# Moving two reloads, one normalization and the opening of an attention stage inside a hand-ordered four-layer graph kernel

## The chip, the cores and the metric

The kernel runs on one core of a Trainium2 chip, as one launch, in float32 throughout. The metric is the device time of one execution in microseconds (us). A core has a matrix engine (PE, with its weight loads shown apart as PEld), a vector engine (DVE), a scalar engine (ACT), a general engine (POOL) and a queue that mainly issues DMA transfers (SP). Each takes its instructions in the order in which the program lists them, and they wait for one another through semaphores.

## The reference, cut to what matters

The input x has 128 batches of 64 tokens with 256 features. Four layers follow one another. Each begins with a layer norm and a relu and adds its result to x:

```python
# layer 0: aggregation with a normalized adjacency, then two dense layers with batch norms
x = x + gnn0(relu(layernorm(x)), adj, W1, ..., W2, ...)
# layer 1: two graph convolutions, then LSTMs over windows of 1, 2, 3, 4 tokens
h = relu(einsum('ts,bsh->bth', adj, relu(layernorm(x)) @ Wg0 + bg0))
h = relu(einsum('ts,bsh->bth', adj, h @ Wg1 + bg1))
for p in range(1, 5):
    last = lstm_last(Wih[p-1], Whh[p-1], ..., windows of p tokens of h)
    h = h.at[:, every p-th token, :].set(last)
x = x + h
# layer 2: causal attention with one head; layer 3: attention with four heads, masked by adj
x = x + attention2(relu(layernorm(x)), Wqkv, Wo)
x = x + attention3(relu(layernorm(x)), W, adj)
```

The four LSTMs run one after the other: that of length 2 reads what that of length 1 wrote. Layer 0's batch norms need sums over the whole batch, so layer 0 ends everywhere before layer 1 begins anywhere.

## The kernel before, in words

The 8192 tokens are cut into 16 chunks of 512 (`NCH`), and two chunks make a superchunk (`SUP`), of which there are 8, numbered 0 to 7. Most large products are done with seven block products in place of eight, with sums and differences of blocks on DVE and POOL; that is where names such as `xd` (differences of an operand) and `hd` come from.

Three stretches follow one another. The first is layer 0. The second, from about 240 us to about 1525 us of the profile, is layer 1: one superchunk at a time goes through the LSTMs of length 1, 2, 3 and 4 (`single`, line 1346, and `lstm`, line 1072). The third is the two attentions.

**The places of a superchunk.** `single` and `lstm` are generators. They list the LSTM's instructions and stop (`yield`) at places where other work may be listed. The loop at lines 1597 to 1632 counts the places of a superchunk from 0 to 21, with half places in between: 0 to 3 are in the LSTM of length 1, 4 to 7 in that of length 2, 8 to 13 in that of length 3 and 14 to 21 in that of length 4. At each place it advances the generators that are due there. Since the engines take instructions in listed order, a place fixes what is ahead of what on every engine.

**What is placed.** `convolutions` (line 1001) prepares a chunk for its LSTMs in 17 steps. In the order of the steps it: scales the stored result of layer 0 (line 918, DVE); transposes it and writes it to memory in HBM (`put`, line 261, into `far_y`); reads it back in another layout (`get`, line 268, four transfers of 128 KB into a `cv` tile) and loads the chunk of x (line 1017, 512 KB into `xs`); adds the two (`add_squares`, line 298, two DVE instructions); takes the layer norm's sums in two halves (`norm_halves`, lines 195 to 203, with the factors on POOL at the end); applies the norm in two halves on ACT (line 210); and goes on with the convolutions' products. The `put` writes out the tile that `xs` then takes over.

`BEGUN` gives the places of the first steps for the two chunks of the superchunk after the next: eight steps for its first chunk, four for its second. `CONV` gives the places of the other steps, one superchunk later; `FIRST` (the tuple at line 1561) does so for superchunk 0, where nothing was begun ahead. The steps of BEGUN run in superchunks 0 to 5, so twelve chunks are begun in this way.

**The queue that they share.** All these transfers, and the LSTMs' weights, are issued by SP in listed order. `load_sets(2)` (line 905) issues two weight sets `wset` of 896 KB each; it stands twice in the last time step of every LSTM of length 2 to 4: between places 11.5 and 12 and again between 12 and 13 for length 3, and between 19.5 and 20 and again between 20 and 21 for length 4. There are six buffers for such sets. `residual` (line 1304) adds the LSTMs' result to x and `ahead` (line 1495) prepares attention; both put and get through SP as well.

**The opening of attention.** After layer 1 the order is written as lists of steps. The string `FIRST` (line 2054) opens it: its entries name a step and a chunk, as `score2+2` is the masked score of layer 2 for chunk 2, `divide2`, `turn2` and `out2` are the softmax's division, its transposes and the product with v, `norm3`, `apply3` and `chan3` are layer 3's norm sums, its application (with one DVE instruction, line 185, and four on ACT, line 187) and the transposes to channels, `q30`, `k30`, `q31`, `k31` are layer 3's projections (line 1529), and `res1` and `pair1` are the last steps of layer 1's residual for chunks 14 and 15. `THIRD` follows, with the first round of the steady order.

Of the kernel before, what the change touches and what calls it, by code (L numbers as in the profile page):

```python
# [19 lines left out]
def kernel(  # L20
# [1443 lines left out]
    def new_hT(sc):  # L1464

        hTs[sc] = l1r.tile([P, KD, SUP * CH], F32, tag="hT", name=f"hT_{sc}")
# [89 lines left out]
    EARLY = 0, 3, 5, 7, 9, 9, 13, 15  # L1556
    RESIDUAL = (0, 6, 9), (5.5, 7, 9.5)
    CONV = (3, 4, 5, 5.5, 7, 8, 9, 10, 10), (5, 5, 6, 9.5, 11, 11.5, 13, 14, 15, 15.5, 17, 18, 20)
    BEGUN = (11, 11.5, 13, 14.5, 17, 17, 20, 21), (17.5, 19, 20, 21)
    RESIDUAL_LAST = (0, 4, 5.5), (3, 5, 9)  # L1560
    FIRST = (0, 1, 1, 1, 2, 3, 4, 4, 5, 5.5, 7, 8, 9, 10, 10), (2, 3, 4, 5, 5, 5.5, 6, 9.5, 11, 11.5, 13, 14, 15, 15.5, 17, 18, 20)
    AHEAD = (9, 10), (10, 11)
    LATE = (4.5, 4.5, 5.5, 9, 19.5), (9.5, 9.5, 11, 12, 21)
    LATEST = (4.5, 4.5, 5.5, 9, 9.5), (9.5, 9.5, 10, 11, 11.5)
# [27 lines left out]
    with tc.manual_schedule(engines={mybir.EngineType.PE, mybir.EngineType.DVE, mybir.EngineType.Pool,  # L1592
# [4 lines left out]
        for sc in range(last + 1):  # L1597
            todo = {}

            def units(places, unit):  # L1600
                for n in places:
                    todo.setdefault(n, []).append(unit)


            if sc < last:
                for i in range(SUP):
                    units((CONV if sc else FIRST)[i], convs[(sc + 1) * SUP + i])
                new_hT(sc + 1)
# [11 lines left out]
            if sc + 1 < last:  # L1620
                for i in range(SUP):
                    units(BEGUN[i], convs[(sc + 2) * SUP + i])
            if sc == last:
# [406 lines left out]
    def store(c, t):  # L2030
# [3 lines left out]
        for r in range(2):  # L2034
# [17 lines left out]


    FIRST = """load2+2 score2+0 exp2+0 v2a+1 v2b+1 divide2+0 score2+1 turn2+0 load2+3 v2a+2 exp2+1 res1+14
               out2+0 keep+0 weights3+0 q2+2 norm3+0 divide2+1 v2b+2 copyq2+2 turn2+1 score2+2 apply3+0 back+0
               out2+1 keep+1 exp2+2 chan3+0 divide2+2 res1+15 res1+14 turn2+2 norm3+1 out2+2 keep+2 q30+0
               k30+0 res1+15 q31+0 k31+0 apply3+1 res1+14 res1+15 pair1+14 square3+1 score3+0 norm3+2
               pair1+14 pair1+15 v3a+0 load3+1 v3b+0 pair1+15"""
    LAST = """exp3-2 sum3-2 load3+0 divide3-2 qa-1 q5-1 c11-1 v3a-1 qb-1 c12-1 qc-1 turn3-2 qd-1 out3-2
              score3-1 q30+0 store-2 back-1 k30+0 back+0 exp3-1 q31+0 sum3-1 k31+0 divide3-1 score3h+0  # L2060
# [4 lines left out]
    def run(order, c):  # L2065
        for name in order.split():
            i = max(name.find("+"), name.find("-"))
            steps[name[:i]](c + int(name[i:]))

    with tc.manual_schedule(engines={mybir.EngineType.PE, mybir.EngineType.DVE,  # L2070
                                     mybir.EngineType.Activation, mybir.EngineType.Pool,
                                     mybir.EngineType.SP}):
        run(FIRST, 0)
        close_l1r()
# [61 lines left out]
```

## Time and profile before

| what | us |
|---|---|
| median of three runs | 1899.44 |
| lowest and highest of them | 1892.75 and 1899.92 |
| the profiled execution, its own time | 1895.84 |
| its span on the core | 1894.1 |
| PE busy | 1840.2 (97% of the span) |
| DVE busy | 1318.7 (70%) |
| ACT busy | 1048.1 (55%) |
| POOL busy | 608.5 (32%) |

The profile is one execution. A group of instructions is named by line, engine, operation and tile, and has its idle time beside it: how long its engine stood still before it, and what ended that. The chain of work that ended last is followed back from the last instruction to whatever released each step, so a transfer in it counts from its issue. Granted clock is the share of full speed at which PE was allowed to run. PE is busy nearly all the time; what another engine does late costs time only where PE then stands still, or runs slower.

### The profile page before, as it was taken

Reading aid. Unit: us, or ns where it says so; the run is one execution under the profiler, and the core shown is the slowest. Engines: PE = TensorE matmul, PEld = TensorE weight load, DVE = VectorE, ACT = ScalarE, POOL = GpSimd, SP = SyncE. Lnnn points to the kernel's source line nnn. Section 1 sums busy time; section 2 is a strip of 40 time slices with the busy share of each in tenths; the row PEclk is TensorE's granted clock in tenths of the full one; section 3 lists DMA queues with packets and bytes.
Section 4 is the critical chain, followed back from the end, with each engine's and each line's share of the span. In section 5 each row is a group of like instructions: output and inputs, shape, how many; then the busy total and the mean of one; then the engine's idle time right before and its main releaser. Section 6 shows DMA issues by size and latency. Waiting matters only on the chain.

```text
span 1894.1 us, 40658 instructions
## 1 busy us (share of the span) xinstructions
PE 1840.2 (97%) x15463; PEld 1511.4 (80%) x15463; DVE 1318.7 (70%) x3408; ACT 1048.1 (55%) x2499; POOL 608.5 (32%) x856
## 2 busy tenths in 40 slices
PE   8999999999999999999999999999999999999998
PEld 6877856986997897799699689779969867777776
DVE  6768856676666777776776677677567666776776
ACT  5766545556546555565564655656565544444453
POOL 5856623123213222222322322232132213332332
PEclk9999999999999999999999999999999999999999
DMA  3224552123433344242343434424144145454433
GB/s 114 79 63 148 209 202 77 64 88 123 156 112 123 112 156 134 73 154 76 123 156 112 145 112 157 145 76 156 47 148 136 71 140 168 142 150 145 136 113 113
DMA packets 113410, 234.48 MB, mean 124 GB/s; under 512 B 11712, under 2 KB 77120, under 8 KB 113216
## 3 DMA queue, kind: packets, MB, share of 16 engines
q1 hardware_dynamic: 112320, 230.02, 37.6%
q8 instruction: 123, 2.02, 0.4%
q0 software_dynamic: 320, 1.05, 0.2%
q10 hardware_dynamic: 576, 0.82, 0.1%
q14 instruction: 71, 0.58, 0.1%
HBM read 164.21 MB, written 67.63 MB: 122 GB/s over the span
## 4 chain that ended last, share of the span: by engine, by line
PE 80%; DMA 6%; DVE 6%; ACT 3%; issue 2%; SPq 2%; POOL 2%; DVEq 0%; ACTq 0%; POOLq 0%
PE x L1188 21%; PE z L1188 10%; PE y L1188 6%; DMA xs<-in_x_dram 6%; PE v L1522 5%; PE y L1135 3%; PE x L1370 3%; PE p_q L1529 3%; PE X L1826 3%; PE x L1135 2%; PE X L437 2%; PE v L936 2%; PE u L950 2%; PE X L513 2%; PE y L1370 1%
## 5 line engine op out<-in xcount | busy, mean ns | idle before, releaser
L1103 ACT ACTIVATE l_gates<-l_gates,bias 128x256 f32<-128x256 f32 (+4 forms) x528 | 238.1, 498 | 212.5 <-DVE l_gates L1197 110.0
L1188 PE MATMUL x<-xd,wset 128*128 128x128 f32 (+2 forms) x1152 | 255.0, 303 | 0.8 <-ACT l_gates L1194 0.8
L1188 PE MATMUL x<-l_hd,wset 128*128 128x128 f32 (+2 forms) x1152 | 254.6, 303 | 0.0
L1254 POOL TENSOR_TENSOR l_gates<-l_gates 128x512 f32<-128x512 f32 (+2 forms) x48 | 75.2, 1567 | 376.7 <-ACT l_gates L1103 376.7
L1188 PEld LDWEIGHTS x<-xd,wset 128*128 128x128 f32 x1152 | 187.7, 191 | 6.5 <-issue 1.4
L1188 PEld LDWEIGHTS x<-l_hd,wset 128*128 128x128 f32 x1152 | 187.8, 191 | 5.0
L1197 DVE TENSOR_TENSOR l_gates<-l_gates,x 128x128 f32<-128x128 f32 (+2 forms) x384 | 121.2, 321 | 92.2 <-PE x L1188 89.4
L1197 DVE TENSOR_TENSOR l_gates<-l_gates,z 128x128 f32<-128x128 f32 (+2 forms) x384 | 102.4, 318 | 104.4 <-PE z L1188 104.4
L1188 PE MATMUL z<-l_hs,wset 128*128 128x128 f32 (+2 forms) x768 | 147.6, 305 | 6.5 <-DVE l_hs L1112 6.5
L1188 PE MATMUL z<-hT,wset 128*128 128x128 f32 (+2 forms) x768 | 146.3, 303 | 0.0
L1194 ACT COPY l_gates<-y 128x128 f32<-128x128 f32 (+2 forms) x192 | 53.0, 289 | 135.4 <-PE y L1188 127.9
L1188 PEld LDWEIGHTS z<-l_hs,wset 128*128 128x128 f32 x768 | 116.7, 191 | 12.6 <-DVE l_hs L1112 9.2
L1188 PEld LDWEIGHTS z<-hT,wset 128*128 128x128 f32 x768 | 117.1, 191 | 3.3
L1103 ACT ACTIVATE l_gates<-x,bias 128x128 f32<-128x128 f32 (+2 forms) x216 | 84.6, 392 | 28.7 <-PE x L1188 26.0
L1188 PE MATMUL x<-hT,wset 128*128 128x128 f32 (+2 forms) x384 | 85.8, 305 | 0.0
L1370 PE MATMUL x<-xd,wih 128*128 128x512 f32 x144 | 68.5, 622 | 17.6 <-DVE l_gates L1394 17.6
L1188 PE MATMUL x<-l_hs,wset 128*128 128x128 f32 (+2 forms) x384 | 84.9, 303 | 0.0
L327 POOL TENSOR_TENSOR xd<-hT 128x128 f32<-128x128 f32 (+2 forms) x72 | 42.2, 586 | 127.7 <-DVE hT L1114 113.8
L1188 PE MATMUL y<-l_hd,wset 128*128 128x128 f32 (+2 forms) x384 | 83.2, 309 | 0.0
L1188 PE MATMUL y<-xd,wset 128*128 128x128 f32 (+2 forms) x384 | 81.6, 304 | 0.0
L1269 ACT ACTIVATE l_gates<-l_cell 128x256 f32<-128x256 f32 (+2 forms) x144 | 55.3, 384 | 45.8 <-DVE l_cell L1268 45.3
L1644 POOL TENSOR_TENSOR s<-s,mx 128x256 f32<-128x256 f32 (+2 forms) x33 | 40.4, 1224 | 122.8 <-DVE mx L1643 120.0
(356 smaller groups left out, 4547.0 us busy)
## 6 DMA issues: line engine op xcount, KB each, us to landing
wset<-wfar SPq DMA_DIRECT2D x96, 896.0 KB, 7.2
hT<-far_h SPq DMA_DIRECT2D x124, 128.0 KB, 3.8
far_h<-hm SPq DMA_DIRECT2D x16, 512.0 KB, 2.9
far_n<-xs SPq DMA_DIRECT2D x16, 512.0 KB, 3.3
xs<-far_n SPq DMA_DIRECT2D x64, 128.0 KB, 2.8
far_x<-xs SPq DMA_DIRECT2D x16, 512.0 KB, 2.9
x<-far_x SPq DMA_DIRECT2D x64, 128.0 KB, 3.3
xt<-in_x_dram SPq DMA_DIRECT2D x15, 512.0 KB, 3.8
```

The source lines that it names most:

```text
L327: return [lambda: engine.tensor_tensor(t1, b12, b11, OP.subtract), lambda: ((third or engine).tensor_tensor(t3, b22, b12, OP.subtract), en ...
L1103: nc.scalar.activation(gate(q, c, part), src, AF.Tanh if q == 2 else AF.Sigmoid, bias=bs[:, q * KD + c : q * KD + c + 1])
L1135: nc.tensor.matmul(folded(self.psum(kind)), wsets[p, self.q][:, BLOCKS[kind][0], :], ox[0][kind], start=kind in (1, 5), stop=True, skip_gr ...
L1188: nc.tensor.matmul(folded(self.psum(kind)), wsets[p, self.q][:, BLOCKS[kind][i], :], (ox[self.s] if part == "x" else oh)[kind], start=firs ...
L1194: nc.scalar.copy(gate(self.q, kind // 5, halves[kind // 5]), self.psum(kind))
L1197: nc.vector.tensor_add(gate(self.q, *dst), gate(self.q, *a), self.psum(kind))
L1254: nc.gpsimd.tensor_mul(gates[:, 0, :, :n], gates[:, 0, :, :n], gates[:, 2, :, :n])
L1269: nc.scalar.activation(gate(2, c, part), cells[:, c, part], AF.Tanh)
L1370: nc.tensor.matmul(folded(ps(g, kind)), single_block(KINDS1[kind])[:, g, :], right[kind], start=kind in (2, 5, 1), stop=True, skip_group_c ...
L1522: nc.tensor.matmul(ps[:, i, :], hT[:, k, j, :], w[:, k, first : first + D], start=(k == 0), stop=(k == KD - 1))
L1529: nc.tensor.matmul(ps.rearrange("p (a n) -> p a n", n=P), w[:, k, m * P : (m + 1) * P], hT[:, k], start=(k == 0), stop=(k == KD - 1))
L1826: nc.tensor.matmul(st[c, tag][:, i * CH // 2 : (i + 1) * CH // 2].rearrange("p (a n) -> p a n", n=P), w, st[c, "o7"][kind], start=first an ...
```

## The change

Three of the hand-written orders change, and nothing that is computed.

In BEGUN the third step of both chunks, which is the `get` and the load of x, moves to an earlier place: from 13 to 12 for the first chunk and from 20 to 19.5 for the second. In the program's SP order the five transfers of the first chunk now stand ahead of the second pair of weight sets of that time step (and behind the first pair), and those of the second chunk stand ahead of the first pair (and so ahead of both). Nothing else changes in the order of these steps.

In the tuple FIRST, for chunk 2 in superchunk 0, the second half of the norm's sums and the factors move from place 1 to place 2, and the first half of the norm's application moves from 2 to 3. On DVE two of four pairs of `bn_stats` and `bn_aggr` go behind six sums of the LSTM of length 1 (line 1394) and its next products; on POOL the four instructions of the factors go behind the second cell product (line 1380); on ACT all four applications stand together.

In the string FIRST the opening of attention is listed in another order. On PE the score of chunk 2 goes ahead of the transposes of chunk 1's attention, the channel transposes `chan3+0` go ahead of `out2+1`, and `q30` and `k30` go ahead of chunk 2's transposes and output product. On DVE the copy of q (line 1703) goes ahead of chunk 1's division; the norm's factor (line 185) goes ahead of chunk 2's mask (lines 1723 and 1643); the sums of `norm3+1` go ahead of the transposes of `res1+15` (line 1310). On ACT the four applications of the norm go ahead of chunk 1's copy (line 1667).

```diff
-    BEGUN = (11, 11.5, 13, 14.5, 17, 17, 20, 21), (17.5, 19, 20, 21)
+    BEGUN = (11, 11.5, 12, 14.5, 17, 17, 20, 21), (17.5, 19, 19.5, 21)
...
-    FIRST = (0, 1, 1, 1, 2, 3, 4, 4, 5, 5.5, 7, 8, 9, 10, 10), (2, 3, 4, 5, 5, 5.5, 6, 9.5, 11, 11.5, 13, 14, 15, 15.5, 17, 18, 20)
+    FIRST = (0, 1, 1, 2, 3, 3, 4, 4, 5, 5.5, 7, 8, 9, 10, 10), (2, 3, 4, 5, 5, 5.5, 6, 9.5, 11, 11.5, 13, 14, 15, 15.5, 17, 18, 20)
...
-               out2+0 keep+0 weights3+0 q2+2 norm3+0 divide2+1 v2b+2 copyq2+2 turn2+1 score2+2 apply3+0 back+0
-               out2+1 keep+1 exp2+2 chan3+0 divide2+2 res1+15 res1+14 turn2+2 norm3+1 out2+2 keep+2 q30+0
-               k30+0 res1+15 q31+0 k31+0 apply3+1 res1+14 res1+15 pair1+14 square3+1 score3+0 norm3+2
+               out2+0 keep+0 weights3+0 q2+2 norm3+0 copyq2+2 divide2+1 v2b+2 apply3+0 back+0 score2+2 turn2+1
+               chan3+0 out2+1 keep+1 exp2+2 q30+0 k30+0 divide2+2 norm3+1 res1+15 res1+14 turn2+2 out2+2
+               keep+2 res1+15 q31+0 k31+0 apply3+1 res1+14 res1+15 pair1+14 square3+1 score3+0 norm3+2
```

## The prediction

> **What bounds the kernel now.** I read four views, from the whole to the place. The first is the chain that ended last, by line.
>
> ```profile
> by line: PE x L1188 21.0%; PE z L1188 10.5%; PE y L1188 5.5%; DMA xs<-in_x_dram 5.5%; PE v L1522 5.1%; PE y L1135 3.4%; PE x L1370 3.2%; PE p_q L1529 2.8%; PE X L1826 2.6%; PE x L1135 2.2%; PE X L437 2.1%; PE v L936 2.1%; PE u L950 2.0%; PE
> ```
>
> It is a chain of matmuls with one foreign body: the load of x into xs, 5.5% or some 104 us. That counts each load from its issue, while PE worked, so it shows where to look and not what is lost. The losses are in PE's own waits, longest first (first lines).
>
> ```profile
> PE x L1370 <- DVE l_gates L1394: 17.6, 7, 3.7
> PE z L1188 <- DVE l_hs L1112: 6.5, 6, 2.0
> ...
> PE tr L1663 <- DVE s L1654: 2.1, 3, 1.4
> PE x L1135 <- ACT l_gates L1375: 1.7, 1, 1.7
> ```
>
> The first two are 24.1 us, far more than any other. What DVE was late for is in DVE's waits: eleven stops of the add at line 298 until a load of x has landed.
>
> ```profile
> DVE xs L298 <- DMA xs<-in_x_dram: 33.7, 11, 4.8
> ```
>
> The timeline of SP, DVE and PE at two begun chunks shows how a stop becomes PE's.
>
> ```profile
> 374.53 0.32 SPq L261 DMA_DIRECT2D far_y<-ym  x1
> 374.94 5.68 SPq L905 DMA_DIRECT2D wset<-wfar  x4
> 380.72 2.44 SPq L268 DMA_DIRECT2D cv<-far_y  x4
> 383.21 0.44 SPq L1017 DMA_DIRECT2D xs<-in_x_dram  x1
> 394.46 1.29 DVE L298 TENSOR_TENSOR xs<-xs,cv 128x512 f32<-128x512 f32 x2 [3.30 <-DMA xs<-in_x_dram]
> 397.05 1.16 PE L1188 MATMUL z<-l_hs,wset 128*128 128x128 f32 x8 [1.99 <-DVE l_hs L1112]
> ...
> 738.75 1.19 SPq L905 DMA_DIRECT2D wset<-wfar  x2
> 740.35 2.22 SPq L268 DMA_DIRECT2D cv<-far_y  x4
> 742.61 0.55 SPq L1017 DMA_DIRECT2D xs<-in_x_dram  x1
> 752.25 1.29 DVE L298 TENSOR_TENSOR xs<-xs,cv 128x512 f32<-128x512 f32 x2 [4.22 <-DMA xs<-in_x_dram]
> 754.29 4.51 PE L1370 MATMUL x<-xd,wih 128*128 128x512 f32 x6 [3.13 <-DVE l_gates L1394]
> ```
>
> At 374 us four weight sets (3.7 MB) go ahead of the reload, at 738 us two. DVE stops for 3.30 and 4.22 us, PE for 1.99 and 3.13. Over the stops of the first chunks PE loses DVE's stop less about 1.3 us (3.30 gives 1.99, 2.27 gives 0.95, 0.98 gives none), at the second chunks less about 1.1. In the last line six matmuls take 4.51 us; the same six take 2.81 after a wait of 1.54.
>
> [...]from 376 to 386 us the engines move 366 GB/s, the weights, and from 386 to 392 us 218 GB/s, the reload.[...] waits of 3.13 and 3.04 us (at 754 and 1226 us) were followed by 4.51 us in place of 2.81; those of 3.12 and 3.71 us were not.
>
> **First part, the reloads.** Nothing is added or removed; twelve times five transfers move past weight sets on SP.
>
> Second chunks. In superchunk 3 (735 us) SP puts far_y at 735.20 and another 512 KB at 738.31, then weights, reload, weights. Two weight sets are 1.83 MB, at 366 GB/s 5.0 us. Without them ahead, x lands at about 747 rather than 752.1 us; DVE is ready for it at 752.25 − 4.22 = 748.0. The next three such loads come out likewise (906.6 against 907.0; 1063 against 1064; 1219 against 1220 us). In superchunks 1 and 2 SP could issue the reload only when far_y had landed, at 428.7 us, as before; moving 1 MB at 210 GB/s takes 5 us and the last landing some 1.5 more, so about 436.5, where DVE is ready at 436.8. All are just in time, with PE's 1.1 us to spare. PE gets back 1.54 + 1.63 + 3.13 + 3.71 + 3.12 + 3.04 = 16.2 us (the second of these, at 597.75 us, behind a stop that the profile calls issue), and two cold bursts, 2 × (4.51 − 2.81) = 3.4 us.
>
> First chunks. The put at 374.53 lands about 3 us later, so SP issues the reload from 377.6 us, with one pair of weights ahead and the other behind. 0.5 MB of put, 1.8 MB of weights at 366 GB/s (to about 382) and 1 MB at 215 GB/s (to about 387), and 2.3 us from there to the add, as before (392 to 394.4): 389.3 us, where DVE is ready at 391.2. PE gets back 1.99 + 0.95 + 0.72 + 1.47 + 0.69 + 0 = 5.8 us.
>
> The price is that weight sets come later. Pairs moved behind are for length 2 of the next superchunk. At 738.75 us that is line 1135 at 767.6 us; they landed at about 747 and will at about 752. SP also stops for the put to land with the second pair behind it; that pair was issued at 379.74 and now at about 381, for use 70 us later. Both are hidden, by 15 us and more. Were that cover gone, each late pair would cost up to the 5 us that it moves.
>
> Sum: 16.2 + 3.4 + 5.8 = 25.4 us. A check from another side: from one superchunk's line 1370 burst to the next takes 154.9, 158.2, 157.8, 156.5, 157.1 us (starts 448.23, 603.14, 761.38, 919.17, 1075.71, 1232.84), and 151.8 in superchunk 6, which begins no chunk. The excess over 151.8 is 25.7 us, and 3.5 us of waits lie in front of 448 us. So 29 us is the ceiling.
>
> **Second part, superchunk 0.** PE waits 1.43 us at 292.80 for line 1394, which stands behind four pairs of sums on DVE; two pairs (1.1 us) go away, and PE gains 1.15. Next it waits 1.70 us at 298.17 for ACT's line 1375, behind two applications of 1.08 us; they go too. But POOL now runs the four factors (290.36 to 292.31, 1.95 us) just ahead of line 327, whose result PE needs at 298.71. With two sums ending at 295.6, factors 295.65 to 297.6 and line 327 at 1.1, PE gets it at 298.7, as before. So the wait moves to POOL. I take 0.2 us gained; the ends are 0.5 lost (four applications, 2.1 us, now all end at 300.5, right at the aggregation) and 1.5 gained.
>
> **Third part, the opening.** From 1539.8 to 1546.6 PE waits 0.65 and three times 0.16 for ACT's norm, 1.44 for line 1654 and 0.52 for a copy, and then runs cold: its first four p_q matmuls take 3.67 us, the next four 1.72. With the factor before the mask ACT starts at 1537.4 in place of 1539.2; listing every engine's order again with the page's durations, I find q30 and k30 done at 1544.7 and k31 at 1550.3 rather than 1555.4: 5.1 us. But not all of it lasts. Line 1310 for chunk 15 (2.1 us on DVE) is now behind the sums of norm3+1 and ends 2.4 us later, at 1547.8; its put, its reload on SP (behind another put) and so the add at line 298 follow: the add ends at about 1557.3, not 1558.7. PE's next wait, for the DMA of hT at 1569.99, hangs on that add through line 286, a put and a reload. So 1.3 to 2 of the 5.1 us stay; I take 1.5, with 2 lost[...] and 5 gained as ends.
>
> **Sum.** 25.4 + 0.2 + 1.5 = 27.1 us. From the profiled execution's 1895.84 (span 1894.1 and 1.7 around it) that gives 1868.7. The median shown is 3.6 above that execution; taking the middle between 1868.7 and 1899.44 − 27.1 = 1872.3, I predict 1870.5.
>
> **Rivals.** (a) Half comes back: the engines serve the later weights along with the reload, or the freed time meets the next late thing in the same place, as POOL's products at line 1254 and 1380 or the residual's put. For it: second chunks have a margin of 0.3 to 1 us only, and POOL waits on ACT everywhere there. Against it: the one first chunk with a stop of 0.98 us (1175 us) shows PE without any wait. Half of 25.4 and nothing elsewhere: 1896 − 13 = 1883. (b) The change does not do what it says: the reload's start is set by the put's landing, not by its place, so x lands as before. For it: at 428.73 us SP issues it when the put has landed, and does so in both orders. Against it: the bytes ahead. It gives 1895 to 1897. (c) Slower: weight sets become the wait, at line 1135 of length 2. It decides once sets land over 15 us later than now, which needs SP held at the put for that long; then up to 5 us in six superchunks, 30 us lost against 25 gained: 1901 to 1905. The median landing of 7.2 us for a set speaks against it.
>
> **How the numbers follow.** Chances: forecast 0.75, (a) 0.16, (b) 0.05, (c) 0.04. About 0.5%, 9.5 us, is what a measurement here can tell from no change. The forecast's own range is 1862 to 1878, from the ceiling of 29 us with 5 from the opening down to 20 us. The full range goes to 1884 for (a), and to 1861. Faster is the forecast and nearly all of (a): 0.90; same 0.06; slower 0.04.
>
> **What would show it.** Right: no stops of line 298 over 1 us for xs in superchunks 0 to 5; PE's wait for line 1394 down from 17.6 to under 2 us and for line 1112 under 1; no 4.51 us burst; superchunks of about 152 to 153 us. In superchunk 0 a wait of PE for POOL at line 327 appears. In the opening k31 ends 5 us sooner, then PE waits 2 to 4 us more for the hT transfer. Wrong: stops of line 298 that remain and end with the cv reload (first part, landing times), PE waiting on wset, or superchunks still over 155 us with no stop at 298.

## The result and the profile after

The changed kernel takes 1868.99 us (median of four runs, 1867.41 to 1869.69). The kernel before took 1899.68 us beside it (four runs, 1892.75 to 1902.33). The ratio is 0.9843, with a 95% interval from 0.9816 to 0.987. The forecast was 1870.5. The profiled execution has a span of 1867.2 us where before had 1894.1, 26.9 us less.

PE's waits of the kernel after, longest first (total us, times, longest):

```profile
PE s L1720 <- DVE q L1703: 3.5, 1, 3.5
PE z L1135 <- POOL xd L327: 3.1, 1, 3.1
...
PE x L1135 <- ACT l_gates L1375: 0.7, 1, 0.7
PE z L1188 <- DVE l_hs L1112: 0.7, 1, 0.7
...
PE x L1370 <- DVE l_gates L1394: 0.4, 1, 0.4
```

The two long rows of before, 17.6 us for line 1394 and 6.5 for line 1112, are down to 0.4 and 0.7. Two new waits stand at the top, each for one event: one in superchunk 0 (line 327), one in the opening of attention (line 1703). In DVE's waits the eleven stops of line 298 for `xs` are gone. What is left of line 298 are two stops of the opening:

```profile
DVE xs L298 <- DMA hT<-far_h: 4.3, 2, 2.3
```

The timeline of SP, DVE and PE at the second begun chunk of the third superchunk that begins chunks (the prediction calls it superchunk 3), where before SP issued the reload at 740.35, DVE stopped for 4.22 us and PE for 3.13:

```profile
729.65 0.32 SPq L261 DMA_DIRECT2D far_y<-ym  x1
732.75 0.32 SPq L261 DMA_DIRECT2D far_n<-nm  x1
733.25 2.24 SPq L268 DMA_DIRECT2D cv<-far_y  x4
735.55 0.42 SPq L1017 DMA_DIRECT2D xs<-in_x_dram  x1
736.06 2.54 SPq L905 DMA_DIRECT2D wset<-wfar  x4
...
742.41 2.52 DVE L298 TENSOR_TENSOR xs<-xs,cv 128x512 f32<-128x512 f32 x2
...
745.67 2.81 PE L1370 MATMUL x<-xd,wih 128*128 128x512 f32 x6
```

All four weight sets now come behind the reload. The add begins with no stop in front of it, and the six matmuls of line 1370 take 2.81 us and not 4.51.

A landmark on PE splits the gain by stretches. In the LSTM of length 1 of superchunks 1 to 7 a burst of twelve matmuls at line 1370 stands at the same place in the program. Its starts in the kernel after are 447.10, 598.87, 751.06, 903.19, 1055.33, 1207.46 and 1359.30, so a superchunk takes 151.8 to 152.2 us where it took 154.9 to 158.2. The put of the first begun chunk, before any moved reload, comes at 377.44 and not at 374.53.

| stretch | how it is read | gained, us |
|---|---|---|
| superchunk 0 up to that put | 374.53 to 377.44 | −2.9 |
| from the put to the last landmark | last landmark 25.31 sooner, with the 2.91 | 28.2 |
| from there to the first output product of layer 3 (line 1953) | 197.5 us after the landmark, now 198.0 | −0.5 |
| the rest of attention, not edited | 26.9 less the rows above | 2.1 |

Of the 2.9 us, 0.2 arose before the edit acts: the first matmul of line 1370 stands at 274.39 before and at 274.55 after. The last row is no larger than what executions differ by: from that product of line 1953 to the end the twelve profiles of this document take 309.7 to 312.5 us.

### The profile page after: what moved, and what is told of

It is laid out like the page before. It is cut to its first block, busy times and chain, and to the rows that moved or that the text cites. A ratio compares the mean times of both kernels' runs of the same rounds, so it can differ in the third digit from the quotient of the medians.

```text
span 1867.2 us, 40676 instructions
## 1 busy us (share of the span) xinstructions
PE 1833.0 (98%) x15463; PEld 1510.2 (81%) x15463; DVE 1323.3 (71%) x3408; ACT 1051.1 (56%) x2499; POOL 614.3 (33%) x856
## 4 chain that ended last, share of the span: by engine, by line
PE 89%; DVE 5%; ACT 2%; POOL 2%; issue 1%; DMA 1%; SPq 0%; ACTq 0%; DVEq 0%; POOLq 0%
PE x L1188 22%; PE z L1188 11%; PE y L1188 6%; PE v L1522 6%; PE y L1135 4%; PE x L1370 4%; PE y L1370 3%; PE u L950 3%; PE v L936 3%; PE p_q L1529 3%; PE X L1826 3%; PE x L1135 3%; PE X L437 2%; PE X L513 2%; PE z L1135 2%; PE Y L1826 1%
## 5 line engine op out<-in xcount | busy, mean ns | idle before, releaser
L1524 ACT COPY v<-v 128x512 f32<-128x512 f32 x62 | 36.0, 583 | 68.3 <-PE v L1522 68.3
```

## The experiments

**One part of the change at a time.** Four kernels were run beside the kernel before, which took 1900.81 us (36 runs).

The two entries of BEGUN alone:

```diff
-    BEGUN = (11, 11.5, 13, 14.5, 17, 17, 20, 21), (17.5, 19, 20, 21)
+    BEGUN = (11, 11.5, 12, 14.5, 17, 17, 20, 21), (17.5, 19, 19.5, 21)
```

> Only the two entries of BEGUN are changed (third step 13 to 12 and 20 to 19.5). My theory, that the bytes ahead of a reload on the queue set the stop at line 298, gives all of what the reloads bring: 25.4 us by the recorded waits, 28 us if each gap also costs the overlap of matmuls that it breaks. That is 3 us more than nothing else changed would lose at superchunk 0, so this kernel should stand about 1 us below the full change (1868 us), at 1867 to 1871. The rival that the put's landing sets the reload's start gives no change, 1896 to 1899. The rival that half comes back gives 1883 to 1886. In the profile: no stops of line 298 for xs over 1 us, PE waits for line 1394 about 3 us (the two of superchunk 0 and the ones of the change's other parts remain: 1.43 for line 1394, 1.70 for line 1375).

Measured: 1865.28 us, ratio 0.9814 (0.9794 to 0.9835). That is 3.7 us below the full change, so the reloads bring more than the whole and the other two edits take some of it back. It is also 1.7 us under my range, since I had set it only about 1 us below the full change. The put of the first chunk stands at 374.89 and the last landmark at 1356.72, against 374.53 and 1384.61: 27.9 us and the 0.36 by which this execution was late before the change acts, 28.2. It is the same as in the full change. No stop of line 298 is left.

The tuple FIRST alone:

```diff
-    FIRST = (0, 1, 1, 1, 2, 3, ...
+    FIRST = (0, 1, 1, 2, 3, 3, ...
```

> Only the tuple FIRST is changed (superchunk 0). By the prediction's step: 0.2 us gained. By what the traces of before and after show (POOL's line 100 at 2.38 us, then PE 3.12 us idle for line 327 and a cold burst): 2.7 to 3 us lost, so the put of the first begun chunk (374.53 us before) should come at 377.2 to 377.5, and the time be 2 to 3 us over the kernel before, which by the time alone can hardly be told from no change. If the loss in the changed kernel came from the reloads and not from the tuple, the put stays at 374.5.

Measured: 1904.52 us, ratio 1.0019 (1.0006 to 1.0033). The put stands at 377.70, 3.2 us late, so the loss in superchunk 0 belongs to the tuple and not to the reloads. PE waits 3.1 us for line 327, and line 100 takes 2.38 us, as in the full change. Counted from the first matmul of line 1370 (273.71 here) the put is 3.8 us late, where it is 2.7 in the full change: behind the wait the granted clock is at half for 6.83 us here and for 3.41 us there.

The string FIRST alone (the change's third part):

```diff
-    ... norm3+0 divide2+1 v2b+2 copyq2+2 turn2+1 score2+2 apply3+0 back+0
-    out2+1 keep+1 exp2+2 chan3+0 divide2+2 res1+15 res1+14 turn2+2 norm3+1 out2+2 keep+2 q30+0
+    ... norm3+0 copyq2+2 divide2+1 v2b+2 apply3+0 back+0 score2+2 turn2+1
+    chan3+0 out2+1 keep+1 exp2+2 q30+0 k30+0 divide2+2 norm3+1 res1+15 res1+14 turn2+2 out2+2
```

> Only the string FIRST is changed (opening of attention). My theory: 1.5 us gained, 1.6 by the traces; k31 ends 4.9 us sooner and then PE waits about 3.5 us for the copy of q at line 1703, behind a stop of DVE at line 298 for the reload of chunks 14 and 15. Rival: the loss at that place comes from another part (the reloads), and the opening alone gains the full 5 us. The two differ by 3.5 us, read from the span and from the wait for line 1703.

Measured: 1901.11 us, ratio 1.0003 (0.9992 to 1.0014): no gain to be seen. k31 ends 165.9 us after the last landmark, where it ended 170.9 us after it before, so the 5 us are won; then PE waits 3.6 us for line 1703, with the reloads as they were, so the rival, that the reloads cause this wait, falls. The first product of line 1953 comes 196.8 us after the landmark. With the old string it came at 197.5, 197.4, 196.3 and 198.0 in the profiles of before and of the three other kernels of this group, and with the new string at 198.0 in the kernel after. The string moves this point by less than it varies from one execution to the next. My 1.5 us are not shown, and 1.6 by the traces, as the expectation had it, was such a variation: most of it arose in rounds of attention that the edit does not touch.

The first chunks' reload alone:

```diff
-    BEGUN = (11, 11.5, 13, 14.5, 17, 17, 20, 21), (17.5, 19, 20, 21)
+    BEGUN = (11, 11.5, 12, 14.5, 17, 17, 20, 21), (17.5, 19, 20, 21)
```

> Only the first entry of BEGUN is changed (13 to 12); the second chunks keep their reload at 20. My theory: the two edits add up. The recorded waits of the first chunks are 5.8 us, with the broken overlap about 7 us: 1892 to 1893 against 1899.5. In DVE's waits five or six stops of line 298 for xs remain, about 21 us (those of the second chunks), and PE keeps its wait for line 1394 of about 16 us and loses that for line 1112 (6.5 us). Rival: once the first chunk's reload is early, its weights push the second chunk's further back (or pull it forward), so that the six stops that remain are longer or shorter than before by over 1 us each. If the put's landing set the start, the stops of the first chunks remain.

Measured: 1895.15 us, ratio 0.9968 (0.9954 to 0.9982), so 5.7 us gained where 7 were expected. The stops of the first chunks are gone, and PE's 6.5 us for line 1112 are 0.7. Six stops at line 298 remain (3.73, 2.17, 4.74, 5.26, 5.88, 3.65 us). They are not those of before (3.00, 2.70, 4.22, 4.80, 4.21, 4.14), but they also differ by up to 3.4 us in the kernel with the string alone, where no reload was moved. So that a first chunk's reload pushes the second's is not shown. Whether the two entries add up is not shown either, since the second was not run alone.

**More bytes ahead of the reload.** The changed kernel, with the second chunk's reload behind both pairs of weight sets:

```diff
-    BEGUN = ..., (17.5, 19, 19.5, 21)
+    BEGUN = ..., (17.5, 19, 21, 21)
```

> The changed kernel, but the second chunk's reload at place 21: behind both pairs of weights, in place of ahead of both (and of between the pairs, as in the kernel before). A dose: 1.83 MB more ahead of it than before, 3.67 MB more than in the changed kernel. If the bytes ahead set the stop, x lands about 5 us later than before, near 757 us at superchunk 3, DVE stops there 8 to 9 us in place of 4.2, and PE loses some 7 to 8 us there and at the five others: 40 to 50 us over the changed kernel, 1908 to 1920. If the put's landing set the start, nothing changes: 1869. Should SP reach place 21 only after the weights have been issued and waited for, the loss is larger still.

Measured: 1928.67 us, ratio 1.0146 (1.0114 to 1.0177), 59.5 us above the changed kernel in the same group (1869.15) and more than forecast. The timeline of this kernel at the first and at the third of the six places (SP, and in the last line DVE):

```profile
426.75 0.32 SPq L261 DMA_DIRECT2D far_y<-ym  x1
429.09 6.16 SPq L905 DMA_DIRECT2D wset<-wfar  x4
435.36 2.05 SPq L268 DMA_DIRECT2D cv<-far_y  x4
...
749.72 5.14 SPq L905 DMA_DIRECT2D wset<-wfar  x4
758.92 0.32 SPq L261 DMA_DIRECT2D far_n<-nm  x1
759.34 2.77 SPq L268 DMA_DIRECT2D cv<-far_y  x4
...
768.26 1.29 DVE L298 TENSOR_TENSOR xs<-xs,cv 128x512 f32<-128x512 f32 x2 [9.36 <-DMA xs<-in_x_dram]
```

At the first place the reload follows the weights at once, and the stop is 7.89 us where it was 3.00 with half the weights ahead: 4.9 us for 1.83 MB, the 5 us of the forecast. At the third SP stands from 754.9 to 758.9 before a put of `far_n`, and the reload behind it. There the bytes are no longer alone, which I had not seen when I called this a dose. DVE's six stops add up to 51.9 us and PE's waits for line 1394 to 43.0, where the changed kernel has 0.4. All six bursts behind them take 4.71 to 5.46 us in place of 2.81. The theory that the put's landing sets the start asked for 1869 and is out.

**The first chunk's reload ahead of everything.** The changed kernel with its reload before the first pair of weights too:

```diff
-    BEGUN = (11, 11.5, 12, 14.5, ...
+    BEGUN = (11, 11.5, 11.5, 14.5, ...
```

> The changed kernel, but the first chunk's reload at place 11.5, ahead of both pairs of weights. It tries the slower rival (c): SP stands at the reload until the put has landed (about 3 us) with all four sets behind it, so the first pair lands some 8 us later than in the changed kernel, and it is for length 4, of which the first set is read about 20 us after its issue. Forecast: nothing is gained at line 298 (no stop is left to take away), and PE does not wait for a wset, or under 1 us: 1867 to 1871. By rival (c) PE waits for wset up to 5 us in six superchunks: 1880 to 1900.

Measured: 1893.15 us, ratio 0.9952 (0.9935 to 0.997), 24.0 above the changed kernel. My forecast was wrong, and the slower rival right. PE's longest wait in this kernel is new:

```profile
PE x L1135 <- DMA wset<-wfar: 16.0, 6, 4.2
```

and its timeline at the start of length 4 in superchunk 0 shows the first of the six:

```profile
387.39 0.61 PE L1135 MATMUL y<-hT,wset 128*128 128x128 f32 x4
390.00 0.46 PE L1135 MATMUL x<-hT,wset 128*128 128x128 f32 x2 [2.00 <-DMA wset<-wfar]
```

SP puts at 378.38 and then stands at the reload until 381.11. The weights behind it are issued from 383.43, and PE is ready for a set of them at 388.0, 4.6 us later, but even the quickest of the four takes 6.4 us to land. In the changed kernel the first pair is issued from 377.85, its sets take 5.0 and 6.8 us, and the same matmuls begin at 386.90: 9 us after the issue, with some 2 to 4 to spare. I had put the 9 us at 20. So the place that the change chose stands between two limits: one pair further back is what the kernel before had, one pair further ahead costs nearly the whole gain. After this wait of 2.00 us, and again after that of 4.17 us (at 1014.95), the granted clock was at half for 3.41 us, and bursts of four matmuls took 1.06 in place of 0.61 us. That is a part of why 16.0 us of waits cost 24.

**A mended version.** The tuple keeps the norm's sums and factors where they were and puts only the four applications together. In the opening, the transposes of chunk 15's residual go back ahead of the sums of norm3+1:

```diff
-    FIRST = (0, 1, 1, 2, 3, 3, ...
+    FIRST = (0, 1, 1, 1, 3, 3, ...
...
-    chan3+0 out2+1 keep+1 exp2+2 q30+0 k30+0 divide2+2 norm3+1 res1+15 res1+14 turn2+2 out2+2
-    keep+2 res1+15 q31+0
+    chan3+0 out2+1 keep+1 exp2+2 q30+0 k30+0 divide2+2 res1+15 res1+14 norm3+1 turn2+2 out2+2
+    res1+15 keep+2 q31+0
```

> The change with two of its parts written otherwise. Superchunk 0: the norm's sums and factors stay at place 1 as before, only the applications stand together at place 3. Opening: the transposes of chunk 15's residual (line 1310) go back ahead of the sums of norm3+1, and keep+2 behind the second res1+15. If the tuple's loss is the factors on POOL just ahead of line 327, the put of the first begun chunk comes at about 374 us, some 3 us sooner than in the changed kernel. If the wait at line 1703 hangs on line 1310 for chunk 15, it goes from 3.5 to under 1.5 us, and 2 to 3.5 us are gained. Together 1862 to 1865. If line 1310's place is not the cause, the wait stays at 3.5 us and the time is about 1866.

Measured: 1862.80 us (1861.91 to 1863.12), ratio 0.9797 (0.9771 to 0.9822) to the kernel before, and 6.35 us below the changed kernel. It beats both. The put stands at 373.71. Counted from the first matmul of line 1370 (273.80) it comes 3.0 us sooner than in the changed kernel and 0.2 sooner than before. The first product of line 1953 comes 194.6 us after the landmark, 2.9 sooner than before. PE's waits of this kernel at the two places:

```profile
PE x L1370 <- DVE l_gates L1394: 1.4, 1, 1.4
PE s L1720 <- DVE q L1703: 1.4, 1, 1.4
```

The first of them is the wait of before that the tuple was to shorten; leaving it costs 1.4 us, taking it away cost 3.

> The changed kernel once more, on the chip of the other three, to compare them with: 1867 to 1870.

Measured: 1869.15 us, ratio 0.9831 (0.9805 to 0.9857), as in the first measurement.

**What makes line 100 slow.** The changed kernel with one step of superchunk 0 moved, chunk 3's scaling:

```diff
-    ...), (2, 3, 4, 5, 5, 5.5, ...
+    ...), (3, 3, 4, 5, 5, 5.5, ...
```

> The changed kernel, with the scaling of the next chunk (line 918, two DVE instructions) moved from place 2 to place 3, so that it no longer runs on DVE beside POOL's line 100. If line 918 is what makes line 100 slow, line 100 goes from 2.38 back to about 1.04 us, PE's wait for line 327 from 3.12 to about 1.6 us, and the put of the first begun chunk comes some 1.5 us sooner (3 with the cold burst): 1866 to 1867.5. If the multiplications of line 1380 and 1386 on DVE are enough, line 100 stays over 1.8 us, the wait over 2.4, and the time at 1868.5 to 1869.5.

Measured: 1867.41 us (1865.34 to 1868.61). The runs differ by 3.3 us, so the time alone does not decide; the traces do. The timelines of POOL and DVE, first in the kernel after:

```profile
295.71 0.97 DVE L918 TENSOR_SCALAR cv<-z1a,sc_bn,sh_bn 128x512 f32<-128x512 f32 x2
296.40 2.38 POOL L100 TENSOR_TENSOR rstd_b<-rstd_b,mhalf 128x4 f32<-128x4 f32 x1
296.60 0.69 DVE L1380 TENSOR_TENSOR l_gates<-l_gates 128x512 f32<-128x512 f32 x1
297.20 0.69 DVE L1386 TENSOR_TENSOR hT<-l_hs,l_gates 128x512 f32<-128x512 f32 x1
298.05 0.69 DVE L1386 TENSOR_TENSOR hT<-l_cell,l_gates 128x512 f32<-128x512 f32 x1 [0.16 <-ACT l_gates L1383]
...
299.36 0.73 POOL L327 TENSOR_TENSOR xd<-hT 128x256 f32<-128x256 f32 x1
```

and then in this one:

```profile
296.15 1.04 POOL L100 TENSOR_TENSOR rstd_b<-rstd_b,mhalf 128x4 f32<-128x4 f32 x1
296.24 0.69 DVE L1380 TENSOR_TENSOR l_gates<-l_gates 128x512 f32<-128x512 f32 x1 [0.50 <-ACT l_gates L1375]
296.85 0.68 DVE L1386 TENSOR_TENSOR hT<-l_hs,l_gates 128x512 f32<-128x512 f32 x1
297.26 0.34 POOL L202 TENSOR_TENSOR nmr_b<-mv_b,rstd_b 128x4 f32<-128x4 f32 x1
...
297.89 1.11 POOL L327 TENSOR_TENSOR xd<-hT 128x256 f32<-128x256 f32 x1
```

Without line 918 beside it line 100 is back at 1.04 us, although lines 1380 and 1386 run at the same time. PE's wait for line 327 falls from 3.12 to 2.10 us (1.6 were expected), the four matmuls behind it take 1.13 and not 2.08 us, and the put comes at 374.99, 2.45 us sooner. So line 100 was slow only with line 918, a `TENSOR_SCALAR`, beside it. In the kernel after line 100 began at 296.40, while line 918 ran (295.71 to 296.68); line 1380 and two instructions of line 1386 followed on DVE, the last of them until 298.74, and line 100 ended at 298.78. In the later kernel it began before any of them. Line 918 itself took 0.96 us in the kernel before, where POOL's line 327 had begun 0.45 us ahead of it (295.05 and 295.50), 0.95 us in this kernel, again 0.45 us behind line 327 (297.89 and 298.34), and 0.52 us in the kernel after, where it began ahead of POOL's line 99 (295.71 and 295.88). Where one of the two was slow (2.38, 0.96 and 0.95 us) it had begun later than the other, but line 1380 too began later than line 100 in the kernel after (296.60) and took its usual 0.69 us. What the order of arrival does was not tried alone. Lines 202 and 327 on POOL began while line 1386 ran in this kernel and took 0.34 and 1.11 us, where they took 0.20 and 0.73 us in the kernel after.

**Which of the two moves mends the opening.** The mended version with `keep+2` back where the change has it:

```diff
-    res1+15 keep+2 q31+0
+    keep+2 res1+15 q31+0
```

> The mended version with one of its two moves in the opening taken back: the sums of norm3+1 stay behind line 1310 for chunk 15, but keep+2 is ahead of the second res1+15 again, as in the changed kernel. If line 1310's place is the whole cause of the wait at line 1703, that wait stays at 1.4 us and the time at 1862.8. If the place of keep+2 is, the wait goes back to about 3.5 us and the time to 1865.5 to 1866.5.

Measured: 1863.97 us (1863.03 to 1864.28). PE's wait for line 1703 is 1.9 us, so line 1310's place gives at least 1.6 of the 2.1 us by which it fell. The 0.5 us left for `keep+2` are not shown to be its own: with the change's string this wait lies between 3.5 and 4.0 us in six executions. The first product of line 1953 comes 195.0 us after the landmark, 0.4 later than in the mended version.

## Why the prediction was right, and where its steps were wrong

The time is 1.5 us under the forecast, and the reason that carries it holds: the weight sets ahead of a reload set the stop at line 298 (the two entries alone give 28 us, a pair more ahead gives back 4.9 us at the stop where nothing else stands in SP's way, and PE no longer waits behind a reload at either line). That nothing but the bytes ahead of it holds a reload was my assumption: where SP stood before a put (754.9 to 758.9, the second chunk's reload at 21) the stop was 9.36 us, against 7.89 at the first place, with the same four weight sets ahead. Superchunks take 151.8 to 152.2 us, just under the 152 to 153 forecast, and line 1394 keeps 0.4 us of PE's waits. Rivals (a) and (b) are out: no stop is left. But three terms of the sum were off. Measured they are 28.2, −2.9 and −0.5, which with the 2.1 from the rest of attention make 26.9, against 27.1 forecast. That they cancelled so well is luck.

**The reloads, 25.4 us.** They gave 28.2. The sum of recorded waits misses a part. What a superchunk lost against the changed kernel, beside the waits and cold bursts recorded in it before:

| from landmark to landmark, before | longer than after | waits | cold burst | rest | waits counted |
|---|---|---|---|---|---|
| 448.23 to 603.14 | 3.14 | 0.95 + 1.63 | | 0.56 | 2 |
| 603.14 to 761.38 | 6.05 | 0.72 + 3.13 | 1.70 | 0.50 | 2 |
| 761.38 to 919.17 | 5.66 | 1.47 + 3.71 | | 0.48 | 2 |
| 919.17 to 1075.71 | 4.40 | 0.69 + 3.12 | | 0.59 | 2 |
| 1075.71 to 1232.84 | 5.00 | 3.04 | 1.70 | 0.26 | 1 |

The rest is 2.4 us for nine waits, 0.27 each. The mis-sized term is the price of a wait: it is the recorded idle time and about 0.27 us for the matmuls on its two sides, which otherwise overlap in the record (six of 0.59 us stand in 2.81). For eleven waits that is 3.0 us, and 28.4 in all. The ceiling of 29 us, read from the superchunks and not from the waits, had it nearly right.

**Superchunk 0, 0.2 us gained.** It lost 2.9, outside the ends that I gave (0.5 lost, 1.5 gained). The step that failed is "factors 295.65 to 297.6". The waits for lines 1394 and 1375 fell as worked out (1.43 to 0.40 and 1.70 to 0.72), and the wait moved to POOL at line 327, but the factors took from 295.88 to 299.4. I took 1.04 us for line 100 from a place where DVE ran other work, and moved it beside line 918, where it takes 2.38. PE then stood 3.12 us, and behind it ran at half clock for 3.41 us (from 299.61): four matmuls in 2.08 and two in 1.06 us, in place of 1.03 and 0.59.

**The opening, 1.5 us gained.** Nothing can be seen of it: 0.5 lost in the kernel after and 0.7 gained with the string alone, where executions with one string differ by 1.7. k31 came 4.9 us sooner, as forecast. The step that failed is the add that "ends at about 1557.3, not 1558.7". The kernel after has (SP, DVE and then PE):

```profile
1522.51 0.34 SPq L261 DMA_DIRECT2D far_h<-hm  x1
1522.89 2.23 SPq L268 DMA_DIRECT2D hT<-far_h  x4
...
1528.08 1.29 DVE L298 TENSOR_TENSOR xs<-xs,hT 128x512 f32<-128x512 f32 x2 [2.00 <-DMA hT<-far_h]
1531.65 1.30 DVE L298 TENSOR_TENSOR xs<-xs,hT 128x512 f32<-128x512 f32 x2 [2.29 <-DMA hT<-far_h]
...
1538.76 0.66 DVE L1703 COPY q<-p_q 128x512 f32<-128x512 f32 x1
...
1539.47 1.98 PE L1720 MATMUL s<-hT,q 128*64 128x64 f32 x30 [3.55 <-DVE q L1703]
1541.38 3.78 PE L1522 MATMUL v<-wg_sb,hT 128*128 128x256 f32 x8
```

The late put of chunk 15 (1522.51) also holds the reload of chunk 14, which is listed behind it on SP. I had followed chunk 15 alone. DVE stops at both adds, the second ends at 1532.95, which is 1558.3 on the clock of before, and all that DVE has behind it is late with it. The first of it that PE needs is the copy of q at line 1703, and not the hT transfer that I named. Behind the 3.55 us PE ran at half clock: line 1522's eight matmuls take 3.78 us here and 1.99 in the kernel before. Half clock for 6.83 us, which before began at 1543.33, begins here at 1538.65 (1564.0 on the clock of before); the mended version has none in this stretch. So the path that failed is the one from the add: by the copy of q the 5 us had shrunk to 0.4 (1538.76 is 1564.07 on the clock of before, where it stood at 1564.50). With line 1310 ahead of the sums again, and `keep+2` behind the adds' step, 2.9 us of the 5 are kept in the mended version and 2.5 in the last kernel.

**Rival (c)** did not happen in the changed kernel, but my case against it was weak. I weighed the weights that the change moves back, which still have time to spare: in the kernel after, the four sets issued from 736.06 have landed by 749.92, and line 1135 begins at 757.24. The pair ahead of a first chunk's reload has 2 to 4 us, and whoever moves that reload one pair more has the rival's time: 1893 us and PE waiting at line 1135 six times.

**The base.** From the profiled execution the sum gave 1868.7; I added half of its distance to the median and went to 1870.5. The median above a profiled execution was not an error of measurement. In the 36 runs of the kernel before, times from 1893.70 to 1905.14 us go with mean granted clocks from 0.997 down to 0.991 (correlation −0.83), and 0.006 of PE's 1840 us is 11 us, all of that spread. The changed kernel's runs have 0.997 and lie within 0.6 us in one group (0.996 to 0.997 and 2.3 us in the other), the mended version's lie at 0.999 to 1.000. A reading that fits: what before had above its profiled time was cold clock behind the same waits, and went away with them. In the group where both were run, 1900.88 less 1869.15 is 31.7 us, of which the profile pair shows 26.9. That pair's 26.9 include the 2.1 us in rounds of attention that the edits leave alone.

## What to carry to other kernels

When a load is late on a shared queue, count the bytes ahead of it from the issue to the use, then do the same for every load that it overtakes, the nearest one first: here one pair of weights had over 7 us to spare and another 2 to 4. Price a moved instruction by the row of the place it goes to, with what runs beside it on the other engines there (line 100 took 1.04 us in one place and 2.38 in another), not by the row of the place it comes from. And where waits of some 2 to 4 us stand before matmuls, compare medians of many runs: in the 36 of the kernel before the mean clock went from 0.991 to 0.997, and a profile shows one execution.

## What the runs showed of the hardware

- A POOL operation on 128x4 numbers (line 100) took 1.04 us in the kernels before and scaling later, and 2.38 us in the kernel after, where it began beside DVE's `TENSOR_SCALAR`. The `TENSOR_SCALAR` (line 918) took 0.96 and 0.95 us in the kernels before and scaling later, where POOL's line 327 had begun 0.45 us ahead of it, and 0.52 us in the kernel after, where it came first.
- PE's waits cost about 0.27 us each beside their recorded idle time in these bursts (nine waits of the kernel before), and 0.26 us each at five waits of the kernel with the second chunk's reload at 21.
- In the profiles of before and after PE's granted clock fell to half for 3.41 us or for 6.83, and once more up to the end. The starts of these stretches lie whole numbers of steps of 3.413 us apart: in the kernel before 253.09, 754.85, 1225.89, 1543.33 and 1891.50 (147, 138, 93 and 102 steps), in the kernel after 299.61, 1538.65 and 1866.33 (363 and 96 steps). Between 270 and 1500 us the idle time within one such step went with it, and the length of the wait alone did not. The kernel before, around its waits of 3.13 us (to 754.29) and of 3.71 us (to 913.79); each row has the step, its length, the busy time of PE, PEld, DVE, ACT and POOL, PE's granted clock, the DMA share and GB/s:

```profile
751.44:754.85 3.41, 0.56 (x2) 0.35 (x3) 2.60 (x5) 0.67 (x2) 0.00 (x0) 1.00 1.01 416
754.85:758.26 3.41, 3.41 (x6) 1.35 (x5) 2.65 (x6) 3.41 (x8) 1.28 (x1) 0.50 0.43 173
...
908.45:911.87 3.42, 1.63 (x4) 0.38 (x2) 0.12 (x1) 0.00 (x0) 1.26 (x1) 1.00 1.08 355
911.87:915.28 3.41, 1.49 (x4) 0.81 (x5) 3.41 (x6) 1.60 (x3) 0.19 (x1) 1.00 1.00 410
915.28:918.69 3.41, 3.41 (x10) 1.49 (x9) 2.66 (x6) 3.41 (x8) 1.10 (x1) 1.00 0.38 150
```

The shorter wait leaves PE idle for 2.85 us of one step, and the next is at half clock. The longer one is parted into 1.79 and 1.92 us, and the clock stays full. The wait of 3.04 us (before, to 1225.75) lies almost whole in the step to 1225.89, with 3.05 us of idle time in it, and was followed by six matmuls in 4.51 us. There the three full-clock steps with the most idle time (2.71, 2.85 and 3.05 us) were followed by half clock, and none of the others (1.92 us at most). Outside that stretch 1.33 and 1.74 us of idle time (before, in the steps to 253.09 and to 1543.33) were followed by half clock too, so no one limit fits these two profiles.
